# A four-layer convolution and wavelet kernel: the first group's column stages with both images in one stationary operand of 128 columns, and padded rows of two inputs

## The chip, the cores and the metric

The kernel runs on one core of a Trainium2 chip. The metric is device time in microseconds (us). The profile comes from one execution recorded on the chip. Its engines are PE (TensorE, matrix multiplication), PEld (the weight loads of TensorE, which run beside its matmuls), DVE (VectorE), ACT (ScalarE), POOL (GpSimd) and SP (SyncE, which issues all DMAs here).

## The reference

The input x holds 4 batch images of 64 channels, 256 x 256, in float32. Four layers follow one another:

- Layers 0, 2 and 3 convolve each image with a long filter that is the outer product of one row filter and one column filter per channel, and add the image times a bias of its channel. The filters come from a small network. Since the filter is a product and the result is cut to 256 x 256, a layer is a multiplication by a triangular Toeplitz matrix along the rows and by another along the columns.
- Layer 1 is a two-dimensional Haar transform, a mixing of the channels with a threshold, done twice and summed, and the inverse transform, plus its input:

```
f1 = haar2d(x)
for i in range(2):
    f4 = einsum('bchw,oc->bohw', f1 * v[i], conv_w[i])
    acc += sign(f4) * relu(abs(f4) - tau[i])
x = haar2d(acc, inverse=True) + x
```

## The kernel before

**Tiling.** The batch is cut into two groups of two images. A group has 32 rounds (`ROUNDS`); a round holds two channels of both images, that is four pictures, as a tile of 128 partitions by 8 x 256 (`big`). A picture is cut into 4 blocks (`BLOCKS`) of 64 rows (`ROW`). In the tile that a row stage reads, the two halves of 64 partitions are the two batch images, and the index that follows is the channel.

**Phases.** Phase A (`phase_a`) is layer 0 and the forward Haar transform, 64 rounds. Phase B (`phase_b`) mixes the channels of a group through DRAM tensors; it runs twice, `phase_b(0)` beside the second half of phase A and `phase_b(1)` beside the first 29 rounds of phase C. Phase C (`phase_c`) is the inverse transform and layers 2 and 3, 64 rounds. `beside` deals the pieces of two phases out in one fixed order, by count. Rounds 0 to 31 of phase C belong to the first group; `alone` is 32, and from there on phase C also does part of the threshold (`shrink`).

**A convolution stage.** `rows` and `columns` call `toeplitz` (L289, its matmul is L293) once for each of four blocks j. The picture is the stationary operand and the Toeplitz matrix is the moving one, so that each product comes out turned and the next stage can go along the other axis. The array is used as four tiles of 64 x 64; the result goes to two PSUM tiles (`banks`), one for each half r of the partitions that were read:

```
for k in range(BLOCKS):
    for r, c in TILES:
        nc.tensor.matmul(ps[r][half(c), j % 2, k * ROW :], data[half(r), c, k, bass.ts(j, ROW)],
                         t(r, c)[:, : N - k * ROW], ..., tile_position=(r * ROW, c * ROW))
```

So a block j has 16 matmuls in the code, with moving widths of 256, 192, 128 and 64 (k from 0 to 3). A float32 matmul appears in the profile as two weight loads and two matmuls. After every second j, ScalarE copies the two PSUM tiles of a row stage to SBUF (`ch`, L839 in phase C), and VectorE adds bias times input to those of a column stage (`residual`, L858). After a row stage the halves of the partitions are the two channels and the following index is the batch image. The row filter depends on c (`filters_x`); the column filter depends on r alone (`filters_y`).

**A round of phase C** is 18 pieces: four of `rows` for layer 2 (tile name `c1r`), one `product` (the Haar matmuls `c0ps`, L305), four of `columns` of layer 3 (`c2c`) for the round two before, four of `rows` of layer 3 (`c2r`) for the round before, one `product`, and four of `columns` of layer 2 (`c1c`). Between them lie pieces of `phase_b(1)`, among them `mix` (tile name `f`, L603): 4 matmuls of 512 columns in tiles of 64 x 64. On each engine the order is the one in which the code issues.

**Inputs.** `load_x` (L144) reads x: four DMAs of 256 KB for a round of the first group, one of 1 MB for a round of the second. In DRAM a partition's row of x has 2048 elements, 8 KB, and the next row follows at once. `load_v` (`fetch`, L557) reads v and tau, 8 KB a row in `phase_b(0)` and mostly 4 KB of it in `phase_b(1)`; these rows also follow one another at 8 KB.

Of the kernel before, what the change touches and what calls it, by code (L numbers as in the profile page):

```python
# [41 lines left out]
F32 = mybir.dt.float32  # L42
# [5 lines left out]
P = 128  # L48
B, C, N = 4, 64, 256

ROW = 64
BLOCKS = N // ROW
# [13 lines left out]
GROUPS = 2  # L66
NB = B // GROUPS
CI = 4 // NB
M = CI * NB

ROUNDS = C // CI
HALVES = 2 * ROUNDS
STEPS = C
# [6 lines left out]
W = 2 * N  # L80
# [4 lines left out]
IMAGES = (GROUPS, NB, ROUNDS, CI, BLOCKS, ROW, N)  # L85
TO_ROUNDS = (0, 2, 1, 5, 3, 4, 6)
# [10 lines left out]
def conv_haar_kernel(  # L97
    ctx: ExitStack, tc: tile.TileContext, x, zT, w1, wbd, cols, wo, decay, wo_first, decay_first, bias, forward, inverse, wrow, pack, v, v_rows, out
):
    nc = tc.nc  # L100
# [21 lines left out]
    def big(tag, name, bufs):  # L122
        return ac.tile([P, 2 * M, N], F32, tag=tag, name=name, bufs=bufs)

    def blocks(images):

        return images.rearrange("p (i k) j -> p i k j", i=2)
# [4 lines left out]
    def banks(name):  # L132

        ring = rings[asked[0] % len(rings)]
        asked[0] += 1
        return [ring.tile([P, 2, N], F32, tag="ps", name=f"{name}_{r}") for r in range(2)]

    def load_x(t):
        grp, r = divmod(t, ROUNDS)
        xs = big("in", f"x_{t}", 3)  # L140

        n = CI if grp == 0 else 2 * M
        for k in range(0, 2 * M, n):
            nc.sync.dma_start(xs[:, k : k + n], x[grp, r, :, k : k + n])  # L144
        return xs

    def load_toeplitz(l, t):
# [107 lines left out]
    def spread(l, begin, end, parts):  # L255
# [8 lines left out]
        return [lambda c=c: put(slice(c * n, (c + 1) * n)) for c in range(parts)]  # L264

    first_x = [load_x(0)]
    forward_sb = const.tile([P, ROW], F32, tag="forward", name="forward_sb")
    nc.sync.dma_start(forward_sb, forward)
# [17 lines left out]
    def half(r):  # L286
        return slice(r * ROW, (r + 1) * ROW)

    def toeplitz(ps, data, t, j):  # L289

        for k in range(BLOCKS):
            for r, c in TILES:
                nc.tensor.matmul(  # L293
                    ps[r][half(c), j % 2, k * ROW :],
                    data[half(r), c, k, bass.ts(j, ROW)],
                    t(r, c)[:, : N - k * ROW],
                    start=k == 0,
                    stop=k == BLOCKS - 1,
                    tile_position=(r * ROW, c * ROW),
                )  # L300

    def haar(ps, pairs, matrix):

        for r, c in TILES:
            nc.tensor.matmul(  # L305
                ps[r][half(c)].rearrange("p h k -> p (h k)"),
                matrix[half(r)],
                pairs(r, c).rearrange("p h k -> p (h k)"),
                start=True,
                stop=True,  # L310
                tile_position=(r * ROW, c * ROW),
            )

    def filters_x(toep):
        return lambda r, c: toep[half(r), c * PERIOD : c * PERIOD + N]

    def filters_y(toep):
        return lambda r, c: toep[half(r), CI * PERIOD :]

    def forward_free(src, dst, name):  # L320
# [4 lines left out]
        while half > 0:  # L325
            sums = nxt = None
            if half > 1:
                nxt = ac.tile([P, 2 * M, half], F32, tag=f"h{half}", name=f"{name}{half}", bufs=1)
                sums = nxt
# [18 lines left out]
    def diffs(src, half):  # L348

        if half < BLOCKS:  # L350
            return src.rearrange("p n (k q) -> p n k q", k=BLOCKS)[:, :, half : 2 * half, 0]
        m = half // BLOCKS
        return src.rearrange("p n (k q) -> p (n k) q", k=BLOCKS)[:, :, m : 2 * m]
# [9 lines left out]
    def inverse_free(src, dst, name, engine):  # L363
# [5 lines left out]
        while half < N:  # L369
            o = dst  # L370
            if half < HALF:
                o = ac.tile([P, 2 * M, 2 * half], F32, tag=f"h{2 * half}", name=f"{name}{2 * half}", bufs=1)
            d = diffs(src, half)
# [17 lines left out]
    def later(op):  # L391

        waiting.append(op)
# [11 lines left out]
    def all_rows(grp_tile, r, images, joined):  # L405

        parts = images.rearrange("(m q) (h n) k -> q m h (n k)", q=2, h=2)
        n = NB * W
        pairs = []
        for q in range(2):  # L410
            for h in (slice(0, 2),) if joined else (slice(0, 1), slice(1, 2)):
                at = grp_tile.offset + ((h.start * 2 + q) * ROUNDS + r) * n
                rows = [[PAIR, P // 2], [2 * ROUNDS * n, h.stop - h.start], [1, n]]
                pairs.append((bass.AP(grp_tile.tensor, at, rows), parts[q][:, h]))
        return pairs

    def phase_a():
# [9 lines left out]
        def load(t):  # L427
            if t < total:
                st[t]["x"] = first_x[t] if t < len(first_x) else load_x(t)

        def rows(t, j):
            s = st[t]
            if j == 0:
                s["y"] = big("t0", f"ay_{t}", 2)
            if j % 2 == 0:
                s["ps"] = banks(f"a1ps{j}_{t}")
            toeplitz(s["ps"], blocks(s["x"]), filters_x(s["toep"]), j)
            if j % 2:
                for r, ps in enumerate(s["ps"]):
                    y = blocks(s["y"])[:, r, j - 1 : j + 1]  # L440
                    later(lambda y=y, ps=ps: nc.scalar.copy(y, ps))  # L441
# [79 lines left out]
    def phase_b(grp):  # L521
# [4 lines left out]
        def raw(u):  # L526
            return grp == GROUPS - 1 and u % 2 == 1 and FULL <= u // 2 < STEPS
# [19 lines left out]
        def load_v(s):  # L547
            if s >= STEPS:
                return
            d = st[s]  # L550
            d["v"], d["tau"] = [], []

            def fetch(first, count, tag):
                n = 2 * count * W
                t = bp.tile([P, count, 2, W], F32, tag=tag, name=f"{tag}_{grp}_{first}_{s}", bufs=3)
                at = v.offset + s * P * 4 * W + first * 2 * W
                nc.sync.dma_start(t.rearrange("p i k w -> p (i k w)"), bass.AP(v.tensor, at, [[4 * W, P], [1, n]]))  # L557
                d["v"] += [t[:, i, 0] for i in range(count)]
                d["tau"] += [t[:, i, 1] for i in range(count)]

            fetch(0, 2 if grp < GROUPS - 1 else 1, "v")
            if grp == GROUPS - 1 and not raw(2 * s + 1):
                fetch(1, 1, "raw")
# [169 lines left out]
    def phase_c():  # L733
# [3 lines left out]
        alone = total - ROUNDS  # L737
        st = [dict() for _ in range(total)]

        def load(t):  # L740
            if t >= total:
                return
            st[t]["g"] = big("in", f"g_{t}", 3)
            st[t]["scales"] = scales(st[t]["g"])
            for rows, g in all_rows(mixed[t // ROUNDS], t % ROUNDS, st[t]["g"], False):
                nc.sync.dma_start(g, rows)

        def load_raw(t):
            if alone <= t < total:
                r = st[t]["raw"] = late["sb"].tile([P, 2 * M, N], F32, tag="raw", name=f"raw_{t}", bufs=2)  # L750
                for rows, to in all_rows(unshrunk, t % ROUNDS, r, False):
                    nc.sync.dma_start(to, rows)
# [76 lines left out]
        def rows(t, l, j):  # L829
            s = st[t]  # L830
            if j == 0:
                s["half", l] = big("t0", f"ch{l}_{t}", 2)
            if j % 2 == 0:
                s["ps", l] = banks(f"c{l}r{j}_{t}")
            toeplitz(s["ps", l], blocks(s["y"]), filters_x(s["toep", l]), j)
            if j % 2:
                for r, ps in enumerate(s["ps", l]):
                    y = blocks(s["half", l])[:, r, j - 1 : j + 1]
                    later(lambda y=y, ps=ps: nc.scalar.copy(y, ps))  # L839

        def columns(t, l, j):
            s = st[t]
            if j == 0:
                s["new"] = big("out", f"o_{t}", 2) if l == 2 else big("m0", f"cy_{t}", 2)
            if j % 2 == 0:
                s["ps", l] = banks(f"c{l}c{j}_{t}")
            toeplitz(s["ps", l], blocks(s["half", l]), filters_y(s["toep", l]), j)
            if j % 2:
                new, old = blocks(s["new"]), blocks(s["y"])
                for e, ps in enumerate(s["ps", l]):  # L850
                    later(lambda e=e, ps=ps: residual(t, l, e, j, new, old, ps))
            if j == BLOCKS - 1:
                s["y"] = s["new"]

        def residual(t, l, e, j, new, old, ps):
            at = l * C + t % ROUNDS * CI + e
            to, of = new[:, e, j - 1 : j + 1], old[:, e, j - 1 : j + 1]
            nc.vector.scalar_tensor_tensor(to, of, bias_sb[:, at : at + 1], ps, ALU.mult, ALU.add)  # L858
            if l == 2 and t == total - 1:

                nc.sync.dma_start(blocks(out[t // ROUNDS, t % ROUNDS])[:, e, j - 1 : j + 1], to)
# [96 lines left out]
    a, head = a[-2 * A_PIECES :], A_PIECES + BLOCKS  # L958
# [134 lines left out]
```

## Time and profile before

| | |
|---|---|
| median of 3 runs | 2593.26 us (2591.77 to 2598.52) |
| the profiled execution | 2595.18 us, of which its span is 2591.5 us |
| PE / PEld / DVE / ACT / POOL busy | 90 / 73 / 72 / 51 / 80 % of the span |
| phase A without B | 0 to about 430 us |
| phase A with B of the first group | to about 1118 us |
| phase C with B of the second group | about 1118 to 1868 us |
| phase C alone | about 1868 to 2591 us |
| granted TensorE clock, mean | 0.977 |

The time of the profiled execution is its span and 3.7 us around it. Busy time of PE counts matmuls whose ends are modelled and which overlap, so that the starts of successive matmuls say more than their durations. The limits of the phases are read from the first and last starts of their tiles.

### The profile page before, as it was taken

The numbers are of one execution on the slowest core, as the hardware profiler recorded it, in microseconds if no ns is written. First come the engines' busy times: TensorE is split into PE (matmuls) and PEld (weight loads), VectorE is DVE, ScalarE is ACT, GpSimd is POOL, SyncE is SP. The second block draws the span as 40 slices with busy tenths as digits, with TensorE's granted clock in tenths as the row PEclk, the third lists the DMA queues.
The fourth block names the chain that finished last, engine by engine and source line by source line (L and its number), as shares of the span: only waits on it lengthen the run. The fifth ranks groups of instructions, "written<-read, shape, count | busy, mean of one in ns | idle before, by whom it ended". The sixth has DMA issues, their size and how long they took to land.

```text
span 2591.5 us, 118522 instructions
## 1 busy us (share of the span) xinstructions
PE 2324.7 (90%) x53292; PEld 1892.3 (73%) x53292; DVE 1858.3 (72%) x2049; ACT 1329.6 (51%) x2187; POOL 2067.0 (80%) x2428
## 2 busy tenths in 40 slices
PE   5999998778888888757999999999989999999999
PEld 4887787444454445546777787787889999999998
DVE  2555445799999999646677677667757787777863
ACT  1221112566666666225666666666656556555552
POOL 1898887899999999757676877767779999999991
PEclk8999999999999999978999999999999999999999
DMA  7676898699999999555998989889876666666653
GB/s 209 219 245 232 287 304 293 248 346 317 348 324 329 346 321 331 184 191 184 328 320 304 330 302 313 309 313 315 289 221 219 212 203 222 210 205 210 215 166 112
DMA packets 203676, 685.23 MB, mean 264 GB/s; under 512 B 29289, under 2 KB 30826, under 8 KB 190755
## 3 DMA queue, kind: packets, MB, share of 16 engines
q1 hardware_dynamic: 203171, 677.67, 76.6%
q8 instruction: 418, 6.85, 1.1%
q14 instruction: 87, 0.71, 0.1%
HBM read 427.93 MB, written 249.63 MB: 261 GB/s over the span
## 4 chain that ended last, share of the span: by engine, by line
PE 53%; DVE 17%; POOL 9%; DMA 9%; issue 6%; ACT 3%; SPq 1%; DVEq 0%; ACTq 0%; POOLq 0%
PE c2c L293 9%; PE c2r L293 9%; PE c1r L293 8%; PE c1c L293 7%; PE a1ps L293 6%; PE a2ps L293 5%; PE f L603 4%; PE c0ps L305 3%; DVE m L647 3%; DVE x L622 3%; DMA v<-in_v 3%; POOL fw L341 2%; DVE a L642 2%; POOL f L343 2%; PE a3ps L305 2%
## 5 line engine op out<-in xcount | busy, mean ns | idle before, releaser
L382 POOL TENSOR_TENSOR i<-i,g 128x16 f32<-128x16 f32 x744 | 411.9, 574 | 27.7 <-ACT g L359 0.6
L293 PEld LDWEIGHTS a2ps<-toep,ay 64*64 64x64 f32 x8192 | 309.6, 137 | 158.0 <-DVE f L474 85.5
L293 PE MATMUL a2ps<-toep,ay 64*64 64x128 f32 (+3 forms) x8192 | 357.5, 306 | 46.6 <-DVE f L474 41.8
L603 PE MATMUL f<-ft,mix 64*64 64x512 f32 x2048 | 297.6, 619 | 109.5 <-DVE x L622 96.7
L293 PEld LDWEIGHTS a1ps<-toep,x 64*64 64x64 f32 x8192 | 293.6, 134 | 88.1 <-issue 43.7
L293 PE MATMUL a1ps<-toep,x 64*64 64x128 f32 (+3 forms) x8192 | 339.0, 300 | 18.6 <-DMA x<-in_x 13.8
L293 PEld LDWEIGHTS c2c<-toep,ch 64*64 64x64 f32 x8192 | 309.7, 134 | 54.1 <-issue 19.1
L293 PEld LDWEIGHTS c1c<-toep,ch 64*64 64x64 f32 x8192 | 306.6, 134 | 52.8 <-issue 17.5
L382 POOL TENSOR_TENSOR ci<-i,g 128x1024 f32<-128x1024 f32 x124 | 336.3, 2732 | 4.6
L293 PE MATMUL c1r<-toep,z 64*64 64x256 f32 (+3 forms) x8192 | 320.4, 300 | 19.2 <-ACT z L827 10.8
L293 PEld LDWEIGHTS c1r<-toep,z 64*64 64x64 f32 x8192 | 299.4, 135 | 47.6 <-issue 22.4
L293 PE MATMUL c2c<-toep,ch 64*64 64x128 f32 (+3 forms) x8192 | 320.7, 299 | 9.6 <-ACT ch L839 6.5
L293 PE MATMUL c1c<-toep,ch 64*64 64x192 f32 (+3 forms) x8192 | 316.9, 298 | 9.3 <-ACT ch L839 7.0
L441 ACT COPY ay<-a1ps 128x512 f32<-128x512 f32 x256 | 137.4, 589 | 351.8 <-PE a1ps L293 351.2
L293 PE MATMUL c2r<-toep,cy 64*64 64x128 f32 (+3 forms) x8192 | 311.9, 297 | 6.5 <-issue 5.9
L293 PEld LDWEIGHTS c2r<-toep,cy 64*64 64x64 f32 x8192 | 294.2, 134 | 30.5 <-issue 18.8
L665 POOL TENSOR_TENSOR gt<-m,ft 128x512 f32<-128x512 f32 x128 | 163.3, 1276 | 185.5 <-DVE m L647 179.1
L628 ACT ACTIVATE m<-x 128x1024 f32<-128x1024 f32 x194 | 206.1, 1063 | 193.6 <-DVE x L622 86.2
L839 ACT COPY ch<-c2r 128x512 f32<-128x512 f32 x256 | 137.5, 590 | 239.2 <-PE c2r L293 238.9
L474 DVE TENSOR_TENSOR f<-a3ps,wrow_sb 128x512 f32<-128x512 f32 x256 | 161.3, 682 | 132.6 <-PE a3ps L305 132.6
L622 DVE TENSOR_TENSOR x<-f,v 128x1024 f32<-128x1024 f32 x192 | 233.4, 1216 | 21.2 <-PE f L603 20.4
L839 ACT COPY ch<-c1r 128x512 f32<-128x512 f32 x256 | 137.8, 593 | 205.4 <-PE c1r L293 205.0
(83 smaller groups left out, 4001.2 us busy)
## 6 DMA issues: line engine op xcount, KB each, us to landing
toep<-filt SPq DMA_DIRECT2D x384, 224.0 KB, 5.4
ft<-coef SPq DMA_DIRECT2D x128, 512.0 KB, 7.7
v<-in_v SPq DMA_DIRECT2D x64, 1024.0 KB, 9.1
mixed<-gt SPq DMA_DIRECT2D x128, 512.0 KB, 7.4
g<-mixed SPq DMA_DIRECT2D x256, 256.0 KB, 5.3
x<-in_x SPq DMA_DIRECT2D x128, 256.0 KB, 4.9
coef<-f SPq DMA_DIRECT2D x128, 256.0 KB, 4.3
x<-in_x SPq DMA_DIRECT2D x32, 1024.0 KB, 8.6
```

The source lines that it names most:

```text
L293: nc.tensor.matmul(ps[r][half(c), j % 2, k * ROW :], data[half(r), c, k, bass.ts(j, ROW)], t(r, c)[:, : N - k * ROW], start=k == 0, stop=k ...
L305: nc.tensor.matmul(ps[r][half(c)].rearrange("p h k -> p (h k)"), matrix[half(r)], pairs(r, c).rearrange("p h k -> p (h k)"), start=True, s ...
L341: nc.gpsimd.tensor_tensor(diffs, even, odd, ALU.subtract)
L382: engine.tensor_tensor(to, s, d, op)
L441: later(lambda y=y, ps=ps: nc.scalar.copy(y, ps))
L474: later(lambda f=f, ps=ps, w=w: nc.vector.tensor_tensor(f, ps, w, ALU.mult))
L603: nc.tensor.matmul(un[u]["f4"][half(q), b, :], mixers[0][half(r), bass.ts(i, C)], st[s]["f"][half(r), b], start=True, stop=True, tile_posi ...
L622: nc.vector.tensor_tensor(un[u]["x"], un[u]["f4"], both(u, "v"), ALU.mult)
L628: nc.scalar.activation(un[u]["m"], un[u]["x"], AF.Sign)
L647: nc.vector.scalar_tensor_tensor(un[u]["m"], un[u]["a"], 0.0, un[u]["m"], ALU.max, ALU.mult)
L665: nc.gpsimd.tensor_tensor(g[:, 0], m[:, 0], st[s]["f"][:, 0], ALU.add)
L839: later(lambda y=y, ps=ps: nc.scalar.copy(y, ps))
```

## The change

Three things change.

1. For the rounds below `alone` (t < 32), `columns` calls `toeplitz_wide` in place of `toeplitz`: the two tiles of 64 x 64 that share a half r, a moving operand and a PSUM tile become one tile of 64 x 128. A block j then has 8 matmuls in the code, with the same moving widths.
2. For this the results of the row stage of those rounds are laid out in another order. `turn` takes the place of the copy L839: the same ScalarE copy of 128 x 512 out of PSUM, which writes runs of 64 elements, so that the 64 elements of the one batch image and those of the other lie side by side.
3. The rows of x and of v in DRAM get 128 elements (512 B) more, which are not read: the pitch goes from 8192 to 8704 bytes. The host pads them when it lays out the inputs. The output keeps its shape.

```
+PAD = 128
...
-            nc.sync.dma_start(xs[:, k : k + n], x[grp, r, :, k : k + n])
+            at = x[grp, r, :, k * N : (k + n) * N]
+            nc.sync.dma_start(xs[:, k : k + n].rearrange("p n k -> p (n k)"), at)
...
+    def side_by_side(data):
+        return data.rearrange("p n k -> p (n k)").rearrange("p (k j c q) -> p k j c q", k=BLOCKS, j=BLOCKS, c=2)
+
+    def toeplitz_wide(ps, data, t, j):
+        for k in range(BLOCKS):
+            for r in range(2):
+                nc.tensor.matmul(
+                    ps[r][:, j % 2, k * ROW :],
+                    data[half(r), k, j].rearrange("p c q -> p (c q)"),
+                    t(r, 0)[:, : N - k * ROW],
+                    start=k == 0,
+                    stop=k == BLOCKS - 1,
+                    tile_position=(r * ROW, 0),
+                )
+
+    def turn(data, r, j, ps):
+        to = side_by_side(data)[:, j - 1 : j + 1, :, r]
+        nc.scalar.copy(to, ps.rearrange("p i (j q) -> p i j q", q=ROW))
...
-                at = v.offset + s * P * 4 * W + first * 2 * W
+                at = v.offset + s * P * (4 * W + PAD) + first * 2 * W
+                rows = bass.AP(v.tensor, at, [[4 * W + PAD, P], [1, n]])
...
                 for r, ps in enumerate(s["ps", l]):
+                    if t < alone:
+                        later(lambda r=r, ps=ps: turn(s["half", l], r, j, ps))
+                        continue
...
-            toeplitz(s["ps", l], blocks(s["half", l]), filters_y(s["toep", l]), j)
+            if t < alone:
+                toeplitz_wide(s["ps", l], side_by_side(s["half", l]), filters_y(s["toep", l]), j)
+            else:
+                toeplitz(s["ps", l], blocks(s["half", l]), filters_y(s["toep", l]), j)
```

More of the change, by code (lines that the diff above doesn't have):

```diff
@@ L555, in fetch @@
                 t = bp.tile([P, count, 2, W], F32, tag=tag, name=f"{tag}_{grp}_{first}_{s}", bufs=3)
-                at = v.offset + s * P * 4 * W + first * 2 * W
-                nc.sync.dma_start(t.rearrange("p i k w -> p (i k w)"), bass.AP(v.tensor, at, [[4 * W, P], [1, n]]))
+                at = v.offset + s * P * (4 * W + PAD) + first * 2 * W
+                rows = bass.AP(v.tensor, at, [[4 * W + PAD, P], [1, n]])
+                nc.sync.dma_start(t.rearrange("p i k w -> p (i k w)"), rows)
                 d["v"] += [t[:, i, 0] for i in range(count)]
@@ L1021, with padded @@
     w = np.abs(full).max(axis=1)
+    def padded(rows):
+        return f(np.concatenate([rows, np.zeros((*rows.shape[:-1], PAD), np.float32)], axis=-1))
     def ordered(name):
@@ L1046 @@
     arrays = {
-        "x": f(a["x"].reshape(IMAGES).transpose(TO_ROUNDS).reshape(GROUPS, ROUNDS, P, CI * BLOCKS, N)),
+        "x": padded(a["x"].reshape(IMAGES).transpose(TO_ROUNDS).reshape(GROUPS, ROUNDS, P, 2 * M * N)),
         "zT": f(np.stack([a[p + "z"].reshape(N, EMB).T for p in CONV], axis=1)),
@@ L1078 @@
         "pack": f(np.concatenate([pack, pack])),
-        "v": f(np.repeat(v[:, :, None], C, axis=2)),
+        "v": padded(np.repeat(v[:, :, None], C, axis=2).reshape(STEPS * P, 4 * W)),
         "v_rows": f(np.stack([by_block("v"), by_block("tau")], axis=1)),
@@ L1086 @@
     ]
-    args.append(nc.dram_tensor("out", arrays["x"].shape, F32, kind="ExternalOutput").ap())
+    args.append(nc.dram_tensor("out", (GROUPS, ROUNDS, P, CI * BLOCKS, N), F32, kind="ExternalOutput").ap())
     with tile.TileContext(nc) as tc:
```

## The prediction

> **What bounds the kernel now.** The slices of the page come first, then the busy times by stretch, the chain of waits, and last the starts of single matmuls.
>
> ```profile
> PE   5999998778888888757999999999989999999999
> ...
> PEclk8999999999999999978999999999999999999999
> DMA  7676898699999999555998989889876666666653
> ```
>
> From slice 20 on (about 1235 us) PE is at 9 in nearly all slices, with the clock full. DMA is at 9 in the middle too, so the busy times have to decide:
>
> ```profile
> core 0: us, PE busy (x) PEld busy (x) DVE busy (x) ACT busy (x) POOL busy (x), PEclk, DMA share, GB/s
> 1117.80:1235.00 117.20, 84.82 (x1624) 62.79 (x1624) 61.93 (x67) 52.08 (x96) 83.42 (x95) 0.83 0.60 204
> 1235.00:1866.00 631.00, 591.76 (x13964) 493.81 (x13960) 452.96 (x429) 403.97 (x702) 461.15 (x508) 1.00 0.90 314
> ...
> 1950.00:2550.00 600.00, 598.29 (x16230) 567.66 (x16226) 457.11 (x482) 337.00 (x626) 538.58 (x540) 1.00 0.63 203
> ```
>
> The changed column stages run in the second stretch (phase C beside phase B), some in the first. There PE is 94% busy, POOL 73%, DVE 72%, ACT 64%. The chain of waits of that stretch agrees:
>
> ```profile
> by line: PE c2c L293 15.4%; PE c2r L293 15.2%; PE f L603 15.0%; PE c1r L293 13.6%; PE c1c L293 11.0%; issue 6.3%; PE c0ps L305 5.8%; DVE m L647 3.0%; DVE cy L858 2.9%; DVE x L622 2.6%; DMA toep<-filt 2.2%; DVE x L642 1.9%; DVE raw L619 0.9%
> ```
>
> PE lines sum to 76%, with "issue" 82%. So time added to PE here shows up at the end by about 0.8. Next: is a column stage limited by streaming, by weight loads or by the count of instructions?
>
> ```profile
> 1442.13 4.57 PE L293 MATMUL c2r<-toep,cy 64*64 64x256 f32 x128
> 1446.50 1.07 PE L603 MATMUL f<-ft,mix 64*64 64x512 f32 x8
> ```
>
> Four blocks j take 1446.50 - 1442.13 = 4.37 us, 1.09 us each. In the trace a tile of 64 x 64 starts successive matmuls 215, 162, 109 and 56 ns apart at widths 256, 192, 128 and 64, each width twice: 2 x 542 = 1.084 us. So a block is the pure **streaming** time of its moving columns; nothing else shows.
>
> **What the Trainium skill says.**
> - "TensorE: Matmul & The Clock Gate", section "LDWEIGHTS": a load lasts columns / 1.2 ns, whatever the rows; 53 ns for 64 columns, 107 for 128. The trace agrees: the records differ by 57 ns (133 and 190, below), and the first two loads of a 128-column matmul start 108 ns apart (100.518 and 100.626 us), those of a 64-column one 55 ns.
> - The same page, "The mechanism": loads overlap only where the row group differs. The trace disagrees: both column tiles of one row group load within the 56 ns between their 64-wide matmuls. So two 64-column loads side by side cost 56 ns now, and one of 128 columns cannot.
> - "TensorEngine Tiling (Array Packing)", "Key Properties": changing the tiling mode drains the array. The trace agrees (below).
> - "DMA: Bandwidth & Descriptors", "Latency and other measured facts": row pitches of 512 KiB and more, at powers of two, slow copies; 4 KiB of padding mended it, 192 B did not. No run here shows that for 8 KB and 512 B.
>
> **The change, part by part.**
>
> *Streaming.* 16 matmuls of 64 x 64 per block become 8 of 64 x 128 with the same widths, two row tiles in parallel instead of four tiles. Each row half still streams 256 + 192 + 128 + 64 columns, twice. Gain: 0.
>
> *Weight loads.* In the trace the load for a tile's next matmul starts 1 to 7 ns after its current one, so it has that matmul's time to finish:
>
> ```profile
> L293 PEld LDWEIGHTS c1c<-toep,ch x8192: 129/133/228, 1130.3 to 2573.2; 64*64 64x64 f32 x200
> ...
> L192 PEld LDWEIGHTS mlp_ps<-h,wbd_sb x12: 186/190/338, 7.8 to 152.4; 128*128 128x128 f32 x12
> ```
>
> At 108 ns a load still hides behind 215, 162 and 109, not behind the two 64-wide matmuls: 2 x (108 - 56) = 0.104 us per block. There are 32 rounds x 2 layers x 4 = 256 blocks: 26.6 us. Where a run of wide blocks ends, the last load is counted in the switch below; 105 runs x 0.052 = 5.5 off. **+21.1 us.** Upper bound: if the two row halves could not load at once, each of the 8 steps would take 216 ns, 1.73 us a block, +0.64 x 256 = +165. Four 64-column loads run at once today, so I take the former.
>
> *Mode switches.* All of phase C works in 64 x 64 now. Counting in the order of the changed kernel's PE instructions, the wide blocks fall into 105 runs, cut by `mix` (`f`), `product` (`c0ps`) and row stages: 210 switches. The trace of before has such crossings only around the filter network:
>
> ```profile
> 237.48 0.67 PE L293 MATMUL a2ps<-toep,ay 64*64 64x192 f32 x19
> 238.08 0.65 PE L233 MATMUL mlp_out<-h,wo_sb 128*64 128x256 f32 x2
> 238.65 0.66 PE L293 MATMUL a2ps<-toep,ay 64*64 64x256 f32 x8
> ```
>
> Here the rows alone change; the last 64-wide matmul starts at 237.928 and would be done 53 ns later, yet the next load starts at 238.074. Every crossing shows that pause, 91 to 95 ns, and then a load that nothing covers. At 100 and 152 us, from 64 x 64 to 128 x 128 and back, the stream stands still for 199 ns (92 + 107) and 150 ns (95 + 55). A change of columns alone is not shown; I take the same: 105 x 0.349 = **+36.6 us.** Lower bound 0, if it does not count as a change of mode.
>
> *Exposure.* 21.1 + 36.6 = 57.7 us on PE. Times 0.82: **+47 us.** Below: 0.6, if the idle 39 us of PE in the second stretch give way. Above: 1.0. What is queued behind: PE works in order, so `mix` and the next row stage come later, and with them `multiply` on DVE, Sign on ACT and the sums on POOL; none has a way past PE.
>
> *Fewer instructions.* 4096 pairs of load and matmul fewer. "issue" is 6.3% of 631 us = 40 us of the chain, and the pairs are about a fifth of that stretch's: at most -8, more likely 0, because blocks already run at streaming speed. I take 0.
>
> *Turned copies.* 256 ACT copies keep their 512 elements; mean now 593 and 590 ns. ACT is idle 36% of the stretch, and a whole other stage lies between copy and reader, so even +100 ns each (26 us of ACT) stays hidden; without that cover it would cost those 26. I take 0. DVE, POOL and SP keep their order and shapes.
>
> *Padded rows.* In the trace 2 KB packets of x last 104 ns on average before 390 us (median 84), 8 KB packets of x and v 393 ns between 520 and 1040 us (median 309). If padding took all of that excess, DMA time would fall by some 20 us and 52 us. But who waits? PE waits for x 17.4 us in all, two thirds of it in the first 60 us, where x is queued behind other transfers. Between 520 and 1040 us the longest waits are
>
> ```profile
> PEld f L603 <- DVE x L622: 97.6, 85, 1.5
> ACT a L637 <- DVE m L647: 92.8, 77, 2.5
> PE f L603 <- DVE x L622: 69.5, 84, 1.0
> ```
>
> and no DMA is among them; DVE is busy 124.7 of 130 us there. So **-2 us**, at best -17. At worst the offset rows cost +5; Toeplitz rows of 3584 B, with starts off any such grid, move 25.6 B/ns at the median against 26.5 for 8 KB rows, so I expect no loss.
>
> *Sum:* 47 - 2 = +45 us. The profiled execution (2595.2, that is 2591.5 of span and 3.7 around it) would become 2640. It lies 1.9 above the median of the runs, so the median goes from 2593.3 to **2638 us**.
>
> **The rivals.**
> 1. *No drain between 64 x 64 and 64 x 128* (the row split stays). Then only the loads count: 26.6 x 0.82 - 2 = +20, 2613 us. For it: no such crossing is shown. Against: a change of rows alone pays in full. 12%.
> 2. *Padding decides, and the result is faster.* If transfers set the pace of 520 to 1040 us (DMA share 0.94), shorter packets could free DVE's idle 21 us there and PE's 17 us of waiting for x: -38, against +20 from rival 1 with an exposure of 0.6 or less (+16): about 2571. It decides once padding brings more than the PE term. Against: no wait for DMA in that stretch. 6%.
> 3. *The two row halves load one after the other:* +165, plus 37 of switches, times 0.82: 2758 us. 4%.
>
> That the wide blocks are not emitted is excluded by the instruction order: 2048 matmuls with 128 output partitions.
>
> **How the numbers follow.** Main case 78%, with exposure from 0.6 to 1.0 and the padding bounds 2611 to 2656; rivals 12, 6 and 4%. Reaching to rival 1 and a little above the upper end, for a stall that grows beside PE, the range is 2606 to 2664. A measurement tells about 0.3% (8 us) from no change. Faster takes rival 2: 0.06; the same, where a weak rival 1 meets a good padding: 0.05; slower 0.89.
>
> **What would show it.** `c1c` and `c2c` of the first group as 64*128 with loads of about 190 ns; 64-wide matmuls of a row half 108 ns apart; pauses of about 92 ns at both ends of a wide run; a round between 1235 and 1866 us near 27.2 us instead of 25.8 (392 `c0ps` matmuls, 16 a round, in 631 us); phase C alone from 1950 us unchanged. Wrong if a wide block takes under 1.1 us, if the pauses are missing, or if the stretch before 1118 us changes by over 10 us.

## The result, and the profile after

The changed kernel takes 2600.86 us at the median (2598.12 to 2602.78, 12 runs); the kernel before, beside it, took 2594.24 us (12 runs). The ratio is 1.002, with a 95% interval of 1.0008 to 1.0032: slower by 2 to 8 us. Predicted were 2638 us, 45 more than before, in a range of 2606 to 2664. The direction was right, the size far off. Everything below asks where some 38 us went.

**What happened as predicted.** The slices of the page after, in the same 40 stretches:

```profile
span 2600.7 us, 110330 instructions
...
PE   5999998788888788668999999999999999999999
...
PEclk8999999899999999879999999999999999999999
DMA  7676898699999999456989898888766667666643
```

From slice 20 on (1235 us) PE is now at 9 in all slices, with a slightly lower share of DMA. The busy times by stretch of the changed kernel (columns as in the prediction) say how much:

```profile
1117.80:1235.00 117.20, 88.18 (x1374) 65.72 (x1372) 62.49 (x67) 54.79 (x103) 85.45 (x100) 0.85 0.63 222
1235.00:1866.00 631.00, 619.39 (x10660) 468.33 (x10654) 446.46 (x426) 399.56 (x693) 453.36 (x504) 1.00 0.88 309
...
1950.00:2550.00 600.00, 598.14 (x15980) 562.06 (x15976) 458.19 (x482) 340.65 (x631) 543.32 (x542) 1.00 0.65 204
```

PE's busy time between 1235 and 1866 us went from 591.8 to 619.4 us, its instructions from 13964 to 10660, while 24 rounds take only 1.2% longer (the table below). Phase C alone (third row) is as before. The groups of the tile `c1c`, by shape, show the two halves of the kernel side by side (durations are minimum, median and maximum in ns; first and last start in us):

```profile
L296 PEld LDWEIGHTS c1c<-toep,ch x4096: 129/133/135, 1972.8 to 2581.6; 64*64 64x64 f32 x196
...
L313 PEld LDWEIGHTS c1c<-toep,ch x2048: 182/187/335, 1128.6 to 1957.3; 64*128 64x128 f32 x187
L313 PE MATMUL c1c<-toep,ch x2048: 218/322/792, 1128.6 to 1957.4; 64*128 64x256 f32 x48, 64*128 64x64 f32 x47, 64*128 64x128 f32 x46, 64*128 64x192 f32 x46
```

Loads of 187 ns, as expected. The timeline of PE around one wide run (start, duration, shape, count):

```profile
1447.11 1.09 PE L629 MATMUL f<-ft,mix 64*64 64x512 f32 x8
1448.13 1.42 PE L313 MATMUL c1c<-toep,ch 64*128 64x256 f32 x16
1449.48 2.41 PE L296 MATMUL c1r<-toep,z 64*64 64x256 f32 x64
```

The block takes 1449.48 - 1448.13 = 1.35 us in place of 1.09. By single starts in the trace, the first load of a row half is not covered after the crossing (1448.130, the next one 1448.238), so its second matmul starts 320 ns after the first instead of 215. At the end, the load for the second matmul of 64 columns starts at 1449.215, 111 ns after the load before it. Taking 107 ns for this load and 53 for the columns, the matmul is done at about 1449.375 us, and the next stage's first load starts at 1449.478, about 100 ns later. (The trace records the starts of these two matmuls 58 ns apart and their ends 112 ns apart, so here the start of a record says nothing of the load that the matmul still needs.) Inside a run a wide block takes 1.203 us, a block of the kernel before 1.092. Loads and switches cost about what the prediction said.

**What did not.** The waits of PE between 1235 and 1866 us, longest in total first, in the kernel before:

```profile
engine line waited for: us in total, times, longest us
PE f L603 <- DVE x L622: 15.4, 14, 2.3
PE c1r L293 <- issue: 7.6, 9, 1.6
PE c2r L293 <- issue: 5.9, 6, 1.7
PE c2c L293 <- issue: 3.0, 4, 1.4
PE c1c L293 <- issue: 2.2, 4, 0.9
PE f L603 <- issue: 2.0, 1, 2.0
```

and in the changed one:

```profile
PE f L629 <- DVE x L648: 8.5, 13, 1.8
PE f L629 <- PE c1r L296: 1.3, 4, 0.3
PE f L629 <- PE c2c L313: 0.8, 3, 0.3
```

Before, PE stood still for 20.7 us with nothing to wait for that the profile shows ("issue"): 24 pauses, all but one before a matmul of a convolution stage. After, there is none. And the wait of `mix` for VectorE's product `x` is 7 us shorter.

One pause in the timeline of the kernel before:

```profile
1480.24 4.41 PE L293 MATMUL c1r<-toep,z 64*64 64x256 f32 x114
1486.00 0.44 PE L293 MATMUL c1r<-toep,z 64*64 64x128 f32 x8 [1.34 <-issue]
```

The same stage, the same loop over k and j, and 1.34 us of nothing. The only other event that goes with it is a 16 KB packet on the DMA queue for instructions (q8), which began 2.30 us before the pause ended. By the starts there are 22 pauses of over 300 ns between successive matmuls of one stage, 20.5 us in all; 21 of them end 2.2 to 2.6 us after such a packet began, though these packets begin 5.7 us apart on average (110 in 631 us). The 22nd ends 3.95 us after, and its packet took 3.4 us where the others took about 1. So PE seems to be out of instructions there: that is read from the times alone, since the trace has no record of what PE's queue holds. The DMA queues in this stretch, in the kernel before (packets, MB, share of 16 engines):

```profile
q1 hardware_dynamic: 56259, 195.96, 88.5%
q8 instruction: 110, 1.80, 1.2%
```

and in the changed one, with a quarter of the instruction packets gone:

```profile
q1 hardware_dynamic: 55530, 193.36, 87.2%
q8 instruction: 84, 1.38, 0.9%
```

**Where 24 rounds spend their time.** From the starts of `c0ps` I take 24 whole rounds of the changed stretch and set the intervals between starts of matmuls against the pure streaming time of the moving columns, 547.0 us in both kernels:

| us, 24 rounds | before | after |
|---|---|---|
| whole | 613.8 | 621.1 |
| loads that nothing covers | 0 | 20.0 |
| switches (85 runs) | 0 | 29.7 |
| pauses within a stage | 20.2 | 0 |
| pauses between stages | 1.9 | 0 |
| `mix` late | 24.2 | 14.3 |
| rest, gaps under 60 ns | 20.5 | 10.1 |

("`mix` late" counts the whole interval, a part of which the profile draws as busy.) A load at the end of a run is in both rows of the price, 85 x 0.052 = 4.4 us, so the price is 20.0 + 29.7 - 4.4 = 45.3 us, and 38 us of it come back. Where the same sequences of pieces are set side by side in the two traces, the wide runs come out about 50 us longer; the split between the price and the small gaps is good to some 5 us.

### The profile page after: what moved, and what is told of

The parts are those of the page before. It is cut to its first block, busy times and chain, and to the rows that moved or that the text cites. A ratio compares the mean times of both kernels' runs of the same rounds, so it can differ in the third digit from the quotient of the medians.

```text
span 2600.7 us, 110330 instructions
## 1 busy us (share of the span) xinstructions
PE 2366.5 (91%) x49196; PEld 1862.6 (72%) x49196; DVE 1858.9 (71%) x2049; ACT 1329.7 (51%) x2187; POOL 2060.7 (79%) x2428
## 4 chain that ended last, share of the span: by engine, by line
PE 56%; DVE 16%; POOL 9%; DMA 7%; issue 5%; ACT 3%; SPq 2%; DVEq 0%; ACTq 0%; POOLq 0%
PE c2r L296 9%; PE c1r L296 9%; PE c2c L313 6%; PE a1ps L296 5%; PE c1c L313 5%; PE a2ps L296 4%; PE c2c L296 4%; PE f L629 4%; PE c1c L296 4%; PE c0ps L330 4%; POOL fw L366 3%; DMA v<-in_v 3%; DVE x L648 3%; POOL f L368 3%; DVE m L673 3%
## 5 line engine op out<-in xcount | busy, mean ns | idle before, releaser
L296 PE MATMUL a1ps<-toep,x 64*64 64x64 f32 (+3 forms) x8192 | 338.3, 300 | 17.8 <-DMA x<-in_x 16.6
L296 PEld LDWEIGHTS a1ps<-toep,x 64*64 64x64 f32 x8192 | 288.5, 134 | 91.1 <-issue 41.1
L296 PE MATMUL c1r<-toep,z 64*64 64x128 f32 (+3 forms) x8192 | 308.5, 299 | 11.4 <-ACT z L853 10.9
L296 PEld LDWEIGHTS c1r<-toep,z 64*64 64x64 f32 x8192 | 280.6, 134 | 49.5 <-issue 15.8
L296 PE MATMUL c2r<-toep,cy 64*64 64x256 f32 (+3 forms) x8192 | 305.3, 297 | 0.0
L890 DVE SCALAR_TENSOR_TENSOR o<-cy,bias_sb,c2c 128x512 f32<-128x512 f32 x256 | 177.1, 743 | 103.0 <-PE c2c L313 82.8
L890 DVE SCALAR_TENSOR_TENSOR cy<-z,bias_sb,c1c 128x512 f32<-128x512 f32 x256 | 176.7, 741 | 90.2 <-PE c1c L313 79.6
L366 POOL TENSOR_TENSOR fw<-x 128x1024 f32<-128x1024 f32 x64 | 122.2, 1910 | 149.2 <-DVE x L486 136.7
L486 DVE SCALAR_TENSOR_TENSOR x<-x,bias_sb,a2ps 128x512 f32<-128x512 f32 x256 | 179.3, 743 | 73.6 <-PE a2ps L296 56.4
L366 POOL TENSOR_TENSOR fw<-f 128x512 f32<-128x512 f32 (+6 forms) x448 | 195.9, 437 | 31.1
L832 POOL TENSOR_TENSOR g<-g,shrunk 128x1024 f32<-128x1024 f32 x64 | 172.8, 2721 | 47.3 <-ACT g L384 32.3
```

What stands on the lines that cost most here:

```text
L366: nc.gpsimd.tensor_tensor(diffs, even, odd, ALU.subtract)
L486: nc.vector.scalar_tensor_tensor(to, old, bias_sb[:, c : c + 1], ps, ALU.mult, ALU.add)
L832: nc.gpsimd.tensor_tensor(to, to, of, ALU.add)
```

## The experiments

Three theories. **A, instructions:** the price is paid on PE, but the column stages now issue half as many instructions, and the pauses for instructions, which the crowded DMA engines make long, go away. **B, elastic:** PE has slack in this stretch, and any added PE time is mostly taken up by shorter waits, whatever it consists of. **C, padding:** the padded rows give back what the wide stage costs.

### The two parts apart

The first is the kernel before with the padding of x and v alone, the second the changed kernel with `PAD = 0`.

> The kernel before with the padded rows of x and v alone. Three theories of why the change cost 7 us where 45 were forecast. A (instructions): the wide blocks cost PE what was forecast, about 45 us in the rounds of the second stretch, but PE had stood still for want of instructions there, about 20 us, and with half the instructions in the column stages this is gone; waits for VectorE shrink by another 10. B (elastic): the round's pace is set together with other engines, so that any PE time added in that stretch is mostly swallowed by waits. C (padding): the padded rows paid the difference. C expects 30 to 40 us faster than before here; A and B expect within 3 us of before, and 8 KB packets between 520 and 1040 us near 393 ns as before.

> The changed kernel with the padding set to 0, so that only the wide column blocks and the turned copies are left. C expects about +45 us against before; A and B expect the changed kernel's time, +4 to +9 us against before.

Padding alone: 2584.74 us, ratio 0.9964 (0.9951 to 0.9976), 9 us faster. Wide stage alone: 2610.05 us, ratio 1.0052 (1.0039 to 1.0066), 13.5 us slower. The product of the ratios is 1.0016, in the interval of the whole change: the parts add up. Padding is worth more than the 2 us predicted, and than the 3 us that A and B allowed, but it is not the main miss: the wide stage alone costs 13.5 us where 47 were predicted. C falls. The waits of PE between 1235 and 1866 us with padding alone, first three lines:

```profile
PE f L607 <- DVE x L626: 14.7, 17, 2.3
PE c1r L296 <- issue: 11.3, 11, 1.6
PE c2r L296 <- issue: 2.9, 4, 1.0
```

The pauses stay with padding; with the wide stage alone, 0.7 us of them are left in this stretch, at the DMA share of the kernel before (0.90). It is the wide stage that takes them away.

### The instructions back, at the same PE time

The changed kernel, with the row stages of the first group cut finer: 24 matmuls per block in place of 16, with the same moving columns and loads that stay covered. The whole has as many instructions as the kernel before.

```
+SPLIT = ((0, 2, 4), (0, 2, 3), (0, 2), (0, 1))
...
-        for k in range(BLOCKS):
+        for k, cut in enumerate(cuts):
+          for begin, end in zip(cut, cut[1:]):
...
-            toeplitz(s["ps", l], blocks(s["y"]), filters_x(s["toep", l]), j)
+            toeplitz(s["ps", l], blocks(s["y"]), filters_x(s["toep", l]), j, *[SPLIT] * (t < alone))
```

> The changed kernel, in which the row stages of the first group's rounds cut the width 256 into 128 + 128 and 192 into 128 + 64: 24 matmuls a row block in place of 16, the same columns streamed, loads of 64 columns still hidden. A round then has as many PE instructions as in the kernel before, with the PE time of the changed one. A expects the pauses for instructions to come back: 15 to 30 us slower than the changed kernel (2615 to 2630). B expects the changed kernel's time within 3 us.

2637.73 us, ratio 1.0166 (1.0152 to 1.018): 37 us above the changed kernel, where A expected 15 to 30. That it is also what the prediction said for the change itself is chance. The waits of PE in the stretch:

```profile
PE c1r L299 <- issue: 9.6, 9, 2.5
PE f L632 <- DVE x L651: 7.2, 14, 1.5
PE c2r L299 <- issue: 3.3, 5, 1.2
PE f L632 <- issue: 1.3, 2, 1.1
```

The pauses are back, in the row stages, where the instructions are. Over the 24 rounds: 649.0 us, 28 more than the changed kernel; 17 of that are pauses within a stage, and 9 are gaps under 60 ns (that row is 19.4 us, nearly what it was before the change). That is A for the pauses; what makes up the small gaps isn't shown.

### More time on PE with hardly more instructions

The kernel before, in which each stage of the first group in phase C issues the four products of k = 0 for j = 0 twice.

```
-        for k in range(BLOCKS):
+        for n, k in enumerate([0] * again + list(range(BLOCKS))):
...
-                    stop=k == BLOCKS - 1,
+                    stop=k == BLOCKS - 1 or n < again,
```

> The kernel before, in which the first product (width 256) of the first of four blocks is issued twice in every row and column stage of the first group's rounds: 4 times a round, 2 x 215 ns each, 1.72 us a round, 55 us of PE in 32 rounds, with 6% more PE instructions in a round instead of 25% fewer. The first issue's result is overwritten by the second. A (instructions): the pauses for instructions within runs stay near 20 us in the second stretch, waits for VectorE shrink by some 10: +38 us or more against before. B (elastic waits): +5 to +20 us, as the wide blocks alone gave (+13).

2629.76 us, ratio 1.0133 (1.01 to 1.0167). Over the 24 rounds PE streams 588.1 us, 41.1 more, and they take 31.0 more: an **exposure**, the share of added PE time by which the whole gets longer, **of 0.75**. Over all 32 rounds it is lower: about 34 us (26 to 43) for the 55 us added, 0.63. `mix` is late by 13.7 us instead of 24.2, as after the change, but the pauses within a stage stay (21.0 us):

```profile
PE c1r L293 <- issue: 11.5, 13, 1.7
PE c2c L293 <- issue: 4.6, 8, 1.4
PE f L603 <- DVE x L622: 4.1, 8, 0.7
PE f L603 <- issue: 3.0, 3, 1.7
```

So B is right for a quarter of the price in the 24 rounds, and for a good third over the whole kernel. That would still have left some 36 us of 57.7; the wide stage cost 13.5.

### The wide stage in the other group

The changed kernel with the condition turned round (`t >= alone`), so that the wide blocks lie in rounds 32 to 63 of phase C. Padding stays.

> The wide blocks in the rounds of the second group instead of the first, where phase C runs alone, in the changed kernel with its padding. There the kernel before has no pauses for instructions and PE never stops. The price is 256 x 0.104 = 26.6 us of loads, less 64 x 0.052, and 64 runs x 0.349 = 22.3 us of switches: 45.6 us. A expects all of it: +45 against before, less 9 for the padding, +34 to +40. B expects less than half, under +15, if waits are elastic everywhere; if only beside phase B, the same as A.

2628.63 us, ratio 1.0121 (1.0088 to 1.0154). Against padding alone the ratio is 1.0121 / 0.9964 = 1.016, 41 us for the wide stage, where it cost 13.5 in the first group. (Against the kernel before it is 31 us, 23 to 40, where A expected 34 to 40 and B, if waits are elastic everywhere, under 15.) Busy times of phase C alone:

```profile
1950.00:2550.00 600.00, 600.00 (x11734) 505.23 (x11726) 469.21 (x464) 329.46 (x611) 520.94 (x529) 1.00 0.62 195
```

The DMA share is 0.62, and in the kernel before PE has no wait on "issue" here that could go away. Over 25 rounds the price is 20.8 of loads + 17.0 of switches - 2.6 counted twice = 35.2 us, and they take 517.2 us in place of 489.0: exposure 0.80. The prediction's price and its exposure hold, where there are no pauses to win back.

### Less traffic, the same instructions

The kernel before, with `phase_b(1)` keeping v and tau of one step from there on; it leaves out the later reads, so its values are not the reference's.

```
+            if grp == GROUPS - 1 and s > FULL:
+                d["v"], d["tau"] = kept
+                return
...
+            if s == FULL:
+                kept[:] = list(d["v"]), list(d["tau"])
```

> The kernel before, in which phase B of the second group reads v and tau for its first three steps only and uses the third one's for all later steps (so the values are not the reference's): 61 DMAs of 512 KB fewer, 32 of the 198 MB moved between 1235 and 1866 us. If the pauses for instructions come from fetches that are late beside heavy DMA traffic, the pauses within runs fall from 20 us to under 10 and the time by 10 to 25 us. If they come from the rate at which PE uses instructions alone, the pauses stay and the time is within 5 us of before.

2576.4 us, ratio 0.9929 (0.9905 to 0.9954). The stretch's DMA share fell from 0.90 to 0.78. Its DMA queues:

```profile
q1 hardware_dynamic: 49321, 170.35, 77.2%
q8 instruction: 114, 1.87, 1.2%
```

and the waits of PE in it:

```profile
PE f L608 <- DVE x L627: 19.3, 19, 3.0
...
PE c1c L293 <- issue: 1.1, 2, 0.9
PE c2r L293 <- issue: 0.6, 1, 0.6
PE c1r L293 <- issue: 0.2, 1, 0.2
PE c2c L293 <- issue: 0.2, 1, 0.2
```

With as many instruction packets as before, the pauses within a stage are down to 2.1 us in this view (18.7 before). So they take both: a high rate of instructions and a high DMA load. How the load acts isn't shown. A 16 KB packet lasts as long with it as without (1086 ns on average before, 1070 here), and the trace doesn't say when a packet was asked for; that it begins too late is what is left, and is inferred. The 24 rounds take 595.4 us, 18.4 less: the pauses within a stage fell by 16.6, `mix` is late by 4.8 us more, and the rest lies in the pauses between stages and the small gaps.

Phase A of the kernel before shows the same without an edit:

```profile
130.00:260.00 130.00, 130.00 (x3262) 105.42 (x3258) 72.31 (x114) 26.83 (x50) 115.69 (x193) 1.00 0.72 239
260.00:390.00 130.00, 122.62 (x3125) 104.11 (x3118) 62.49 (x95) 23.72 (x44) 109.12 (x190) 1.00 0.92 297
```

In the first row PE never waits on "issue". In the second, with no more matmuls but a DMA share of 0.92, it does so 7 times in its convolution stages, 5.8 us in all. From 520 to 1040 us, at a share of 0.94 but only 6896 matmuls in 520 us, there is none.

### Half of the switches

The changed kernel with another order of `beside`: a list says between which pieces phase B may come, so that no run of four wide blocks is cut. The wide blocks then fall into 64 runs instead of 105.

```
-    beside(main, phase_b(1), len(c_first) + len(a_end) + 2 * BLOCKS, 0)
+    inside = [int(j % C_PIECES not in (5, 6, 7, 14, 15, 16)) for part in order for j in part]
...
+    beside(main, phase_b(1), len(c_first) + len(a_end) + 2 * BLOCKS, 0, inside)
```

> The changed kernel with no piece of phase B dealt out inside a run of four column blocks: 64 runs of four blocks and 128 switches in place of 105 and 210, and otherwise the same work. By the price of a pair of switches (0.349 us, less 0.052 of a load) PE has 12 us less to do. A expects 6 to 12 us faster than the changed kernel (2589 to 2595), since with the pauses gone PE's time counts nearly in full; B expects within 3 us of it. If the bunched pieces of phase B make PE wait for VectorE, it can be slower by 5 to 10.

2611.75 us, ratio 1.0063 (1.0039 to 1.0086): slower than the changed kernel. The switches did fall, from 29.7 to 17.1 us in the 24 rounds, as 36 runs fewer at 0.349 us say (12.6). But the pieces of phase B come closer together, and `mix` is late by 29.4 us instead of 14.3; it waits for VectorE, which by the order of the pieces has less time between two of them:

```profile
PE f L629 <- DVE x L648: 19.3, 26, 2.4
PE f L629 <- issue: 1.4, 1, 1.4
PE f L629 <- PE c2r L296: 1.0, 3, 0.3
```

26 waits in place of 13. A saving on PE was paid back in a wait for DVE.

### Half of the wide blocks

The changed kernel with the condition `t < alone and l == 2`, so that only the column stage of layer 3 is wide in the first group.

> The changed kernel with the wide column stage in layer 3 of the first group alone (half of the wide blocks, padding kept): 54 runs and 108 switches instead of 105 and 210, so about half of the PE price (29 us). If the pauses for instructions shrink in proportion: halfway between padding alone and the changed kernel, 2590 to 2596 us. If half of the instructions saved already ends most pauses: 2582 to 2588. If the pauses stay as long as one layer is in 64 x 64: 2600 or more.

2592.8 us, ratio 1.0001 (0.9987 to 1.0014). Halfway between padding alone and the whole change is (0.9964 + 1.002) / 2 = 0.9992, in the interval: in time the effect is proportional. In its parts it isn't:

```profile
PE f L629 <- DVE x L648: 15.6, 17, 2.2
PE c1r L296 <- issue: 3.1, 5, 1.1
PE f L629 <- PE c1r L296: 2.0, 4, 0.5
PE c1c L296 <- issue: 1.4, 2, 1.2
```

Of the 16.6 us of waits on "issue" in convolution stages that padding alone shows, the first half of the wide blocks already takes 12.1 away, and the wait for `x` doesn't fall until the second half is wide. That the two balance in time is chance.

### Where padding's gain lies

The kernel before with x padded alone, with v padded alone, and with both padded by 4 KB instead of 512 B (`PAD = 1024`).

> The kernel before with only the rows of x padded by 512 B. The padding of both gave -9 us. x is read in phase A, where PE stood still 6 to 15 us in pauses within runs between 264 and 437 us in the unpadded kernels and 4 to 5 us in the padded ones. If the gain comes from x, -6 to -10 us against before; if from v, within 3 us.

> The kernel before with the 512 B between rows of v alone (x as it was). Padding both gave 0.9964 of before, padding x alone 0.9995. If the gain is v's: 0.995 to 0.998 (6 to 10 us less). If it takes both together, or was a matter of where the tensors come to lie: within 3 us of before.

> The kernel before with rows of x and v padded by 4 KB instead of 512 B. If the pad only has to take the rows off their grid of 8 KB: as with 512 B, 7 to 11 us less than before, packets of 8 KB at a mean near 390 ns between 520 and 1040 us. If 512 B was too little to take the excess out of the packets: a mean under 360 ns there, and 10 to 20 us less than before.

| padded | us | ratio | 95% |
|---|---|---|---|
| x by 512 B | 2594.43 | 0.9995 | 0.9983 to 1.0006 |
| v by 512 B | 2587.42 | 0.9976 | 0.9964 to 0.9988 |
| both by 512 B | 2584.74 | 0.9964 | 0.9951 to 0.9976 |
| both by 4 KB | 2589.36 | 0.9970 | 0.9958 to 0.9982 |

Most of it is v's, x by itself shows nothing, and more padding brings no more. What it does is not settled. The packets did not get shorter: 8 KB packets between 520 and 1040 us take 393 ns on average before, 388 with both padded, 390 with v alone and 390 with 4 KB. The prediction tied a gain to the excess of this mean over the median, in the spirit of what the Trainium skill ("DMA: Bandwidth & Descriptors", "Latency and other measured facts") says of row pitches of 512 KiB and more, where 4 KiB more on a pitch of 4 MiB brought the full rate back; at 8 KB no padding here took the excess away. In the one profiled execution of padding alone the gain is spread thin: 4.6 us before phase B begins, 3 us in phase C alone, about 1 us elsewhere; executions of one kernel differ by as much. Of the 4.6 us, 3.7 are shorter waits on "issue" from 260 to 440 us (2.1 us in place of 5.8), but with v alone padded these are 10.6. Between 1235 and 1866 us the waits on "issue" in convolution stages hardly change (16.6 us against 18.7). Longer rows may also move the tensors in DRAM, and no run sets that apart. The cause stays open.

## Why the prediction was wrong

- **Streaming, 0:** right, 547.0 us in 24 rounds in both kernels.
- **Weight loads, +21.1:** right. 192 of the 256 blocks are in the 24 rounds: 20.0 - 4.4 = 15.6 us measured, 21.1 x 0.75 = 15.8 predicted. (By whole blocks inside a run it is 0.111 us each, 0.104 predicted.)
- **Mode switches, +36.6:** right. 85 of the 105 runs cost 29.7 us, 0.35 us each, as predicted. That a change of columns alone costs the pause too was taken from crossings of another kind, and held. Rivals 1 and 3 fall with it.
- **Exposure, 0.82:** somewhat high as a property of PE time, 0.75 and 0.80 in two experiments, 0.63 over the whole of the first. It came from the chain's share of PE and "issue"; what gives way is `mix`, which before is late by 24.2 us in 24 rounds, mostly for VectorE, and after by 9.9 us less.
- **Fewer instructions, 0, at best -8: this step failed.** In 24 rounds the pauses gave 22.1 us (20.2 within stages, 1.9 between), and the gaps under 60 ns some 6 more (10.4, less the 4.4 counted twice), whose cause isn't shown. Two things were wrong. The evidence for 0 was a stretch of four blocks without a gap, and "blocks already run at streaming speed" is true of nearly every block; 20 us sat in 22 of them. And the bound of -8 took the "issue" time of the chain times the share of instructions saved (a fifth; it was nearer a quarter), as if all instructions carried it evenly. It behaves like a queue that runs dry: with half of the blocks wide, three quarters of the pauses are gone, and with all of them wide, none is left. The waits of PE itself, where "issue" stands with 20.7 us next to PE's own lines, had the answer.
- **Turned copies, 0:** right. The copies of the first group take 588 ns at the median, those of the kernel before 591 to 592.
- **Padding, -2, at best -17:** inside its bound, and mis-sized. It measured -9 (6 to 13). That no DMA stood among the longest waits spoke against a gain, and was no proof.
- **The sum.** For the 24 rounds: 45.3 of price, less 22.1 of pauses, 9.9 of `mix` and 6.0 of small gaps is +7.3. Predicted was +47 x 0.75 = +35. For the whole: wide stage +47 predicted, +13.5 measured; padding -2 predicted, -9 measured.
- **Rival 2** named padding as what could turn the sign. With padding at -9 and the wide stage at +13.5 it did not, though the two came nearer to each other than the sum had them. (Its sum took 21 us for VectorE's idle time from 520 to 1040 us; the stretch shows 23.)
- **The signs.** Shapes, loads, pauses at both ends of a run, phase C alone (25 rounds: 489.0 and 488.3 us) and the stretch before 1118 us (2 us shorter) came as written. The 108 ns between 64-wide matmuls show in their loads (111 ns) and ends (112), not in their recorded starts (58). The round did not come: 25.9 us in place of 27.2.

Of the kernels here that compute the reference's result, the fastest keeps the padding and leaves the column stages as they were: 2584.74 us, ratio 0.9964 to the kernel before.

## What to carry to other kernels

Before you price fewer or more instructions at nothing, read the waits of the bound engine for "issue" and look for pauses in the middle of a loop: a block that runs at full speed says nothing about the block in which the queue ran dry. Added time on the bound engine can be sized step by step and still come out at under a third (13.5 us for 47), because the same edit took away stalls in the same place; price what an edit stops issuing with the same care as what it adds. And where fewer switches were bought by bunching the work of another phase, the cost moved into the wait for that phase.

## What the runs showed of the hardware

- PE paused for 0.4 to 1.8 us in the middle of a stage, 21 times in 22 between 2.2 and 2.6 us after a 16 KB instruction packet began, at a DMA share of 0.90. At 0.78, with as many instruction packets, the pauses within a stage fell from 20.2 to 3.6 us in 24 rounds; phase C alone, at 0.63, had no wait of PE on "issue" in spite of a higher rate of PE instructions (16230 matmuls in 600 us, against 13964 in 631). Phase A had none from 130 to 260 us at 0.72, and 7 in the next 130 us at 0.92, with about as many matmuls.
- A run of 64 x 128 tiles between stages of 64 x 64 costs 0.35 us: at each end a pause of 90 to 100 ns and a load that nothing covers. The pause comes with a change of columns alone.
- Padding rows of 8 KB by 512 B left the packets as long as they were (388 ns on average, 393 before), and yet made the kernel 0.36% faster.
